# W2's broadcast rows kept in PSUM, layer 3's statistics from ScalarE, and a new order of the first microseconds, in a four-layer residual kernel

## The chip, the cores and the metric

The kernel runs on one core of a Trainium2 chip. The metric is the device time of one execution in microseconds; the time before is the median of 8 runs. TensorE is called PE, VectorE DVE, ScalarE ACT, GpSimd POOL and SyncE SP, as in the profile.

## What is computed

x has 128 batches of 128 x 512 numbers, adj is 128 x 128, all in float32. Four layers follow each other, each with a residual and a layer norm:

```
layer 0: y = adj @ x[b];  x = norm(x + y @ weight + bias)
layer 1: q, k, v = x Wq^T, x Wk^T, x Wv^T;  rel = adj^T * (q k^T)
         rel = rel / |rel| (by row);        x = norm(x + rel @ v)
layer 2: h = x W;  e = leaky(h a1 + (h a2)^T) * adj;  att = softmax(e)
         x = norm(x + elu(att @ h + beta h))
layer 3: A = adj @ x;  C = A + b;  pre[n, m] = A[m] + (C - A)[n]
         x = norm(x + max over m of relu(pre))
norm(x) = (x - mean) / sqrt(var + 1e-5) over the 512 features
```

Layer 3's maximum is one number per row: max(0, max_m A[m] + b). So layer 3 adds one number to each row of x, and then normalises the row.

## The kernel before

**Groups.** Four batches make a group (G = 4), and there are 32 groups (NG). Layer 1's q k^T is computed as x M x^T with M = Wq^T Wk, made once. The 512 x 512 products (y with weight, x with M, x with Wv^T, z with W, called y, m, v and z) are done for a whole group in seven steps in place of eight, with sums of blocks of both factors: `weight_blocks` (L143) makes the sums of the weights on DVE, once per weight; `left_factors` (L294) makes those of the activations on POOL, per group, four instructions; `product` (L339) issues the steps in the order 1, 2, 6, 5, 7, 3, 4 (ORDER, L290). Their results build up in three PSUM regions (REGION, L291): r0 takes steps 1, 6, 7, 4, r1 takes step 2, r2 takes steps 5 and 3. After each step, `out` (L353) reads the region: ACT copies it to its block of the result after steps 1, 6, 5 and 4, and DVE adds it to a block after 2, 7 and 3 (in the y product DVE adds all seven). A region's next step may not start before it has been read.

**PSUM.** There are eight banks of 128 x 512. Four take turns as `bank` (tag "ps", L82), for single matmuls and transposes: `p_y`, `p_xT`, `p_rel`, `p_o`, `p_s`, `p_eT`, `p_z`, `p_a` and those of the preparation. Four take turns as regions (tag "r", L350). `direct` (L700), the last group's z product, uses four "r" buffers too.

**Order.** All five engines run their instructions in the order of emission (InOrder, L18). The order is written out by hand: each piece is emitted with a time in slots (TABLE, L231), a group is 28 slots behind the one before, and the pieces are sorted by that number (L783). So the layers of neighbouring groups are interleaved: between the steps of one group's m product stand the `p_y` matmuls of the next group, and so on. FIRST (L248) and LAST (L250) replace rows for the first two and the last three groups.

**Around the change.** `dots` (L559) takes, for each batch, two dot products of every row of x2 (layer 1's x before its norm) with the rows W2 a1 and W2 a2: a DVE instruction `scr<-x,wa` that multiplies and accumulates. The rows, broadcast over the partitions, stand in SBUF as `wa` (L138), made by `prepare_rows` (L202) from transposes in PSUM and two ACT copies. `scale_dots` (L574) turns the dots into those of the normalised x, `d`, which `spread` transposes into `p_s`. `residual` (L545) precedes the dots, and `norm` (L375) follows: `ve` on DVE, the power -0.5 on POOL (`rstd`), `nmean` on DVE, and the scaling on ACT. `elu` (L716) does two DVE instructions (`x<-c,x` and `x<-m,x`) and the statistics for each batch.

Layer 3 (L747): `widen` is adj @ x on PE (`p_a`), `top` is the maximum over a row on DVE (`mx`), the bias and relu on DVE (`top<-mx,b_sb`), and the addition to x on ACT (`x<-x,top`). Then `stats` (L368), bn_stats and bn_aggr on DVE, and `norm`.

**The fill.** SP issues adj, four loads of the first x, Wq, Wk, Wv, a, beta, b; ACT issues the loads of weight (`w0_sb`), bias and W (`w2_sb`), L91 to L122. adj is transposed on PE and copied to `adjT` by ACT (L131). `biased` (L428) adds the bias to x on POOL, four instructions per group, ahead of the sums `s_y` of the y product. M is made by `prepare_qk` (L163), 16 matmuls of 128 x 512 in four banks with four ACT copies; `prepare_v` transposes Wv.

Of the kernel before, what the change touches and what calls it, by code (L numbers as in the profile page):

```python
# [13 lines left out]
EPS = 1e-5  # L14
# [15 lines left out]
def kernel(  # L30
# [41 lines left out]
    G = 4  # L72
    NG = B // G
    assert B % G == 0 and K == 4

# [3 lines left out]
    small = ctx.enter_context(tc.tile_pool(name="small", bufs=4))  # L79
    psum = ctx.enter_context(tc.tile_pool(name="psum", bufs=4, space=bass.MemoryType.PSUM))  # L80

    def bank(name):  # L82
        return psum.tile([P, D], FP, tag="ps", name=name)

# [20 lines left out]
    bias_sb = const.tile([P, D], FP)  # L105
    nc.scalar.dma_start(bias_sb, on_all(bias0, D))

# [7 lines left out]
    w2_sb = const.tile([P, K, D], FP)  # L115
    nc.scalar.dma_start(w2_sb, w2.rearrange("(k p) f -> p k f", p=P))
    a_sb = data.tile([P, 2, D], FP, tag="x3", name="a_sb")
# [9 lines left out]
    dve.memset(mhalf, -0.5)  # L127

    adjT = const.tile([P, P], FP)
    pt = bank("p_adjT")  # L130
    pe.transpose(pt[:, :P], adj_sb, ident)  # L131
    act.copy(adjT, pt[:, :P])
    adj_b = adj_sb[:, None, :].to_broadcast([P, G, P])
# [3 lines left out]
    wvT = const.tile([P, K, D], FP)  # L137
    wa = const.tile([P, 2, D], FP)  # L138
    wa_sum = const.tile([P, 2], FP)
    beta_i = const.tile([P, P], FP)  # L140
    beta_b = beta_i[:, None, :].to_broadcast([P, G, P])

    def weight_blocks(w, name, keep=0):  # L143


        def blk(kh, ch):
            return w[:, 2 * kh : 2 * kh + 2, H * ch : H * ch + H]

        t = const.tile([P, 3 + keep, 2, H], FP, name=f"t_{name}")
# [12 lines left out]

    def prepare_qk(c):  # L163

        pm = bank(f"p_m{c}")
        for e in range(K):
            pe.matmul(
                pm,
                wq_sb[:, e, c * P : (c + 1) * P],
                wk_sb[:, e, :],  # L170
                start=(e == 0),
                stop=(e == K - 1),
            )
        act.copy(m_qk[:, c, :], pm)
        if c == K - 1:
            bw["m"] = weight_blocks(m_qk, "m")

# [24 lines left out]
    def prepare_rows():  # L202

        for i in range(2):
            p = bank(f"p_wa{i}")
            for k in range(K):
                pe.transpose(
                    p[:, k * P : (k + 1) * P], col[:, i, k : k + 1].to_broadcast([P, P]), ident
                )
            act.copy(wa[:, i, :], p)  # L210
        dve.tensor_reduce(wa_sum, wa, AX.X, ALU.add, negate=True)
        dve.tensor_scalar(beta_i, ident, beta_sb, None, op0=ALU.mult)
# [14 lines left out]
    def row(at, step, n=G):  # L227
# [9 lines left out]
        move_rel=row(41.2, 0.1), inverse=[42.5], v=row(42, 1, 7), attend=row(50.6, 1),  # L237
        residual=row(51.0, 1), dots=row(54.2, 1.1), norm1=[55.2], scale=[58.8],
        apply1=row(65.4, 0.33),
# [7 lines left out]

    FIRST = {0: dict(turn=row(20.4, 0.3)), 1: dict(y=row(-9.5, 0.3), bias=row(-9.2, 0.3))}  # L248

# [89 lines left out]
    def product(at, name, mul, s, w, c, fresh, begin=None):  # L339
# [4 lines left out]
        def step(i):  # L344
            if i == 1 and begin is not None:
                begin()
            where = REGION[i]
            first = i in (1, 2, 5)
            if first:
                r[where] = psum.tile([P, 2, H], FP, tag="r", name=f"r{where}_{name}")  # L350
            mul(r[where], s["f"][i], bw[w][i], first)
# [262 lines left out]
    def layer2(g, t):  # L614
# [132 lines left out]
    def layer3(g, t):  # L747
        s = {}

        def widen(b):  # L750
            s["a", b] = bank(f"p_a_{g}_{b}")
            pe.matmul(s["a", b], adjT, x3[g][:, b, :], start=True, stop=True)

        def top(b):
# [3 lines left out]
            tp = small.tile([P, 1], FP, tag="top", name=f"top_{g}_{b}")  # L758
# [19 lines left out]
    emit(40.7, prepare_rows)  # L778
    emit(61.0, prepare_2)
    for g in range(NG):  # L780
# [33 lines left out]
```

## Time and profile before

| | us |
|---|---|
| median of 8 runs | 2235.38 (2233.30 to 2239.59) |
| the profiled execution | 2239.59 |
| its span, first to last instruction | 2237.4 |
| mean granted clock of PE | 0.996 |
| PE busy / DVE / ACT / POOL | 2185.5 / 1799.0 / 980.4 / 986.2 |
| DVE `scr<-x,wa` (dots), 256 | 288.0 busy, mean 1.176 |
| DVE bn_stats / bn_aggr, 512 each | 352.1 / 93.2 busy, mean 0.688 / 0.182 |
| DVE `top<-mx,b_sb`, 128 | 27.5 busy, mean 0.215 |
| DVE `ve<-mv`, 126 of 128x4 | 50.2 busy, mean 0.398 |
| ACT `x<-x,top`, 128 | 92.4 busy, mean 0.722 |
| ACT `x<-x,nmean,rstd`, 512 | 385.7 busy, mean 0.807 |
| ACT accumulator read, 128 of `sq` | 24.0 busy, mean 0.187 |
| PE `p_m` (Wq^T Wk), 32 records | 13.9 busy |

All durations are of one execution. A float32 matmul has two records on PE, a transpose one. Records overlap: the starts of two 128 x 256 records are 0.216 apart at full clock, so a step of eight takes 1.73; 128 x 128 records are 0.11 apart, and 0.21 at half clock. The group rows of the page give busy time and mean duration; the chain of waits gives start, length and name of what held up the end; the timeline gives start, length, engine and operation, and in brackets the idle time ahead of a row and what ended it.

### The profile page before, as it was taken

To read this page: it belongs to the slowest core of one execution; us is meant where nothing else is said; L and a number is where in the kernel's file an instruction comes from. 1 tells how busy PE (TensorE), PEld (TensorE's weight loads), DVE (VectorE), ACT (ScalarE), POOL (GpSimd) and SP (SyncE) were. 2 spreads that over 40 slices of the span, in tenths; PEclk is the share of its full clock that TensorE was granted. 3 is DMA by queue.
4 is the path that set the end of the run, shared out by engine and by line. 5 is a ranking of instruction groups with operands and counts; after the bars stand their busy time and mean duration, and the time that the engine had idled before them with its cause. 6 is when DMAs were issued, how large, how long until landed. Compare 5 with 4: busy or idle time off the path is not lost.

```text
span 2237.4 us, 31661 instructions
## 1 busy us (share of the span) xinstructions
PE 2185.5 (98%) x11073; PEld 1842.7 (82%) x11073; DVE 1799.0 (80%) x3534; ACT 980.4 (44%) x1936; POOL 986.2 (44%) x743
## 2 busy tenths in 40 slices
PE   7999999999999999999999999999999999999996
PEld 5888888888888888888888888888888888888873
DVE  4668888778888788888788888788887788887788
ACT  2224444454444444444444444444444444444535
POOL 3435454334444344554344553354543354443322
PEclk9999999999999999999999999999999999999998
DMA  4010222211222201222112222112222112221111
GB/s 166 25 33 18 58 58 62 62 21 47 59 60 62 62 14 54 57 62 62 43 30 57 57 62 62 41 29 59 57 62 62 38 30 59 59 62 43 20 29 57
DMA packets 333294, 115.15 MB, mean 51 GB/s; under 512 B 297424, under 2 KB 297552, under 8 KB 333136
## 3 DMA queue, kind: packets, MB, share of 16 engines
q1 hardware_dynamic: 331936, 110.77, 19.6%
q10 hardware_dynamic: 1200, 2.36, 0.3%
q8 instruction: 89, 1.46, 0.3%
q14 instruction: 69, 0.57, 0.1%
HBM read 39.65 MB, written 33.55 MB: 33 GB/s over the span
## 4 chain that ended last, share of the span: by engine, by line
PE 70%; DVE 24%; issue 3%; POOL 1%; ACT 1%; DMA 0%; DVEq 0%; ACTq 0%; POOLq 0%
PE r_v L26 17%; PE r_y L26 13%; PE r_z L26 13%; DVE x L26 7%; DVE scr L26 7%; PE r_m L26 6%; PE p_z L26 5%; PE p_o L26 5%; PE p_a L26 5%; PE p_rel L26 4%; DVE st L26 3%; DVE tT L26 2%; PE p_y L26 2%; DVE d L26 1%; DVE e L26 1%
## 5 line engine op out<-in xcount | busy, mean ns | idle before, releaser
L26 ACT ACTIVATE x<-x,nmean,rstd 128x512 f32<-128x512 f32 x512 | 385.7, 807 | 187.7 <-DVE nmean L26 187.6
L26 DVE BATCH_NORM_STATS2 st<-x 128x6 f32<-128x512 f32 x512 | 352.1, 688 | 56.6 <-ACT x L26 47.8
L26 DVE SCALAR_TENSOR_TENSOR scr<-x,wa 128x512 f32<-128x512 f32 x256 | 288.0, 1176 | 0.0
L26 POOL TENSOR_TENSOR rstd<-ve,mhalf 128x4 f32<-128x4 f32 (+1 forms) x134 | 145.4, 1085 | 285.8 <-DVE ve L26 279.8
L26 POOL TENSOR_TENSOR x<-x,bias_sb 128x512 f32<-128x512 f32 x128 | 193.9, 1525 | 74.0 <-PE p_y L26 73.3
L26 POOL TENSOR_TENSOR s_x<-xT 128x512 f32<-128x512 f32 x64 | 95.8, 1496 | 258.8 <-DMA xT<-xB 247.9
L26 ACT ACTIVATE x<-x,top 128x512 f32<-128x512 f32 x128 | 92.4, 722 | 229.6 <-DVE top L26 229.3
L26 DVE TENSOR_TENSOR x<-r_y,x 128x512 f32<-128x512 f32 x224 | 151.4, 676 | 27.0 <-PE r_y L26 26.9
L26 ACT COPY c<-r_z 128x512 f32<-128x512 f32 x124 | 71.9, 580 | 221.5 <-PE r_z L26 221.5
L26 ACT COPY yT<-p_y 128x512 f32<-128x512 f32 x128 | 75.1, 587 | 206.5 <-PE p_y L26 206.5
L26 PEld LDWEIGHTS p_y<-adjT,x 128*128 128x128 f32 x1024 | 135.8, 195 | 13.5 <-ACT adjT L26 5.5
L26 DVE SCALAR_TENSOR_TENSOR x<-p_o,rn,x 128x512 f32<-128x512 f32 x128 | 95.9, 749 | 59.9 <-PE p_o L26 56.0
L26 DVE SCALAR_TENSOR_TENSOR x<-m,x 128x512 f32<-128x512 f32 x128 | 132.8, 1037 | 13.6 <-DVE x L26 0.9
L26 PE MATMUL p_y<-adjT,x 128*128 128x128 f32 x1024 | 136.6, 278 | 6.8 <-ACT adjT L26 5.2
L26 PEld LDWEIGHTS p_z<-eT,x 128*128 128x128 f32 x1024 | 133.9, 192 | 8.4 <-DVE x L26 1.2
L26 PEld LDWEIGHTS p_rel<-xT,tT 128*128 128x128 f32 x1024 | 134.1, 191 | 7.4 <-DVE tT L26 0.8
L26 POOL TENSOR_TENSOR s_z<-zT 128x512 f32<-128x512 f32 x31 | 39.4, 1270 | 223.7 <-ACT zT L26 223.7
L26 PE MATMUL p_rel<-xT,tT 128*128 128x128 f32 x1024 | 134.9, 275 | 0.6 <-DVE tT L26 0.6
L26 PE MATMUL p_z<-eT,x 128*128 128x128 f32 x1024 | 134.8, 275 | 0.4 <-DVE x L26 0.4
L26 PE MATMUL p_a<-x,adjT 128*128 128x512 f32 x256 | 131.2, 597 | 3.6 <-ACT x L26 1.9
L26 ACT COPY tT<-r_m 128x512 f32<-128x512 f32 x128 | 75.6, 590 | 132.5 <-PE r_m L26 132.5
L26 PE MATMUL p_o<-v,relT 128*128 128x512 f32 x256 | 130.3, 593 | 0.0
(119 smaller groups left out, 5011.9 us busy)
## 6 DMA issues: line engine op xcount, KB each, us to landing
out_dram<-x SPq DMA_DIRECT2D x128, 256.0 KB, 2.5
x<-in_x_dram SPq DMA_DIRECT2D x31, 1024.0 KB, 5.8
xT<-xB SPq DMA_DIRECT2D x480, 64.0 KB, 2.3
relT<-relB SPq DMA_DIRECT2D x512, 16.0 KB, 1.8
w_sb<-in_L_gnn_weight_dram ACTq DMA_DIRECT2D x1, 1024.0 KB, 6.0
x<-in_x_dram SPq DMA_DIRECT2D x4, 256.0 KB, 7.5
wq_sb<-in_L_gnn_Wq_dram SPq DMA_DIRECT2D x1, 1024.0 KB, 11.4
wk_sb<-in_L_gnn_Wk_dram SPq DMA_DIRECT2D x1, 1024.0 KB, 14.4
```

What stands on the lines that cost most here:

```text
L26: return lambda *args, **kw: self.tc.keep_in_program_order(op(*args, **kw))
```

## The change

Three things are changed together.

1. PSUM is divided anew: three banks for "ps", two buffers for r0 (tag "r0"), one that r1 and r2 share (tag "r12"), and two banks that hold `wa` for good; `prepare_rows` transposes straight into it, without the copies. The dots read `wa` from PSUM. The dots, norm1 and the scale get earlier slots.
2. Layer 3's statistics: ACT squares the normalised x with an accumulated sum (`squares`), does the bias and relu (`top`, on 128 x 1) and sums x + top while it adds them. `spread` makes mean and variance of x + top from the two sums (the sum of squares belongs to an x whose mean is 0), with five DVE instructions and POOL's power. bn_stats and bn_aggr of layer 3 are gone.
3. The fill: eight identity products ahead of adj's transpose and eight behind the copy, which DVE does now; the loads of bias and W are issued by SP; M is made by `product` in seven steps, with Wq itself as the left factor; norm 0, turn and the bias adds of the first groups get other slots; `prepare_2` comes 12 slots earlier.

```diff
-    psum = ctx.enter_context(tc.tile_pool(name="psum", bufs=4, space=bass.MemoryType.PSUM))
+    psum = ctx.enter_context(tc.tile_pool(name="psum", bufs=1, space=bass.MemoryType.PSUM))
     def bank(name):
-        return psum.tile([P, D], FP, tag="ps", name=name)
+        return psum.tile([P, D], FP, tag="ps", name=name, bufs=3)
...
-    nc.scalar.dma_start(bias_sb, on_all(bias0, D))
+    nc.sync.dma_start(bias_sb, on_all(bias0, D))
...
-    nc.scalar.dma_start(w2_sb, w2.rearrange("(k p) f -> p k f", p=P))
+    nc.sync.dma_start(w2_sb, w2.rearrange("(k p) f -> p k f", p=P))
...
+    warm = bank("p_warm")
+    for i in range(WARM):
+        pe.matmul(warm[:, :P], ident, ident, start=True, stop=True)
     pe.transpose(pt[:, :P], adj_sb, ident)
-    act.copy(adjT, pt[:, :P])
+    dve.tensor_copy(adjT, pt[:, :P])
+    for i in range(WARM):
+        pe.matmul(warm[:, :P], ident, ident, start=True, stop=True)
...
-    wa = const.tile([P, 2, D], FP)
+    wa = psum.tile([P, 2, D], FP, tag="wa", name="wa")
...
-    def prepare_qk(c):
-        pm = bank(f"p_m{c}")
-        for e in range(K):
-            pe.matmul(pm, wq_sb[:, e, c * P : (c + 1) * P], wk_sb[:, e, :], ...)
-        act.copy(m_qk[:, c, :], pm)
-        if c == K - 1:
-            bw["m"] = weight_blocks(m_qk, "m")
+    def prepare_k():
+        bw["k"] = weight_blocks(wk_sb, "k", 1, "x2")
+    def prepare_m():
+        bw["m"] = weight_blocks(m_qk, "m")
...
         for i in range(2):
-            p = bank(f"p_wa{i}")
             for k in range(K):
                 pe.transpose(
-                    p[:, k * P : (k + 1) * P], col[:, i, k : k + 1].to_broadcast([P, P]), ident
-                )
-            act.copy(wa[:, i, :], p)
+                    wa[:, i, k * P : (k + 1) * P],
+                    col[:, i, k : k + 1].to_broadcast([P, P]),
+                    ident,
+                )
...
-        residual=row(51.0, 1), dots=row(54.2, 1.1), norm1=[55.2], scale=[58.8],
+        residual=row(51.0, 1), dots=[51.7, 53.8, 54.9, 55.6], norm1=[54.6], scale=[57.2],
...
-    FIRST = {0: dict(turn=row(20.4, 0.3)), 1: dict(y=row(-9.5, 0.3), bias=row(-9.2, 0.3))}
+    FIRST = {
+        0: dict(stats0=row(13.8, 0.02), norm0=[13.95], apply0=row(18.0, 0.1), turn=row(20.4, 0.3)),
+        1: dict(y=row(-9.5, 0.3), turn=row(20.3, 0.3), x_sums=row(22.5, 0.5)),
+    }
...
-                r[where] = psum.tile([P, 2, H], FP, tag="r", name=f"r{where}_{name}")
+                r[where] = psum.tile(
+                    [P, 2, H], FP, tag="r0" if where == 0 else "r12",
+                    name=f"r{where}_{name}", bufs=2 if where == 0 else 1,
+                )
...
-            s["c", b] = psum.tile([P, D], FP, tag="r", name=f"c_{g}_{b}")
+            s["c", b] = psum.tile([P, D], FP, tag="r0", name=f"c_{g}_{b}", bufs=2)
...
+        def squares(b):
...
+            act.activation(scr, x3[g][:, b, :], AF.Square, accum_out=s["sq"][:, b : b + 1])
         def top(b):
...
-            dve.tensor_scalar(tp, mx, b3_sb, 0.0, op0=ALU.add, op1=ALU.max)
-            act.activation(x, x, AF.Identity, bias=tp)
+            act.activation(tp, mx, AF.Relu, bias=b3_sb)
+            act.activation(x, x, AF.Identity, bias=tp, accum_out=s["sum"][:, b : b + 1])
+        def spread(i):
...
+            dve.tensor_scalar(s["mean", i], s["sum"][:, sl], -1.0 / D, None, op0=ALU.mult)
+            dve.tensor_tensor(d, s["mean", i], s["top"][:, sl], ALU.add)
+            dve.scalar_tensor_tensor(d, d, -1.0, d, op0=ALU.mult, op1=ALU.mult)
+            dve.tensor_scalar(s["sq"][:, sl], s["sq"][:, sl], 1.0 / D, EPS, op0=ALU.mult, op1=ALU.add)
+            dve.tensor_tensor(d, d, s["sq"][:, sl], ALU.add)
+            pool.tensor_tensor(s["r"][:, sl], d, mhalf[:, sl], ALU.pow)
+        def shift(i):
+            dve.tensor_tensor(s["mean", i], s["mean", i], s["r"][:, sl], ALU.mult)
...
+        for b in range(G):
+            emit(t["widen"][b] - 0.1, squares, b)
         each(t["top"], top)
-        each(t["stats3"], lambda b: stats(s, f"3_{g}", b, x3[g][:, b, :]))
-        norm(t["norm3"], t["apply3"], s, f"3_{g}", lambda: x3[g])
+        each(t["norm3"], spread)
+        for i in range(len(t["norm3"])):
+            emit(t["apply3"][i * n] - 0.1, shift, i)
+        each(t["apply3"], apply)
...
-    each(row(14.0, 1.0), prepare_qk)
-    each(row(18.0, 0.1), prepare_v)
+    emit(13.74, prepare_k)
+    qk = {"qT": wq_sb}
+    left_factors(row(12.0, 0.1), qk, "qT", "s_x", "q", 1)
+    product(row(14, 1, 7), "qk", by_rows, qk, "k", rows_of(lambda: m_qk), True)
+    emit(20.74, prepare_m)
+    each(row(21.0, 0.1), prepare_v)
     each(row(29.2, 1.8), prepare_dots)
     emit(40.7, prepare_rows)
-    emit(61.0, prepare_2)
+    emit(48.9, prepare_2)
```

More of the change, by code (lines that the diff above doesn't have):

```diff
@@ L73 @@
     NG = B // G
+    WARM = 8
     assert B % G == 0 and K == 4
@@ L141, with weight_blocks @@
     beta_b = beta_i[:, None, :].to_broadcast([P, G, P])
-    def weight_blocks(w, name, keep=0):
+    def weight_blocks(w, name, keep=0, where=None):
         def blk(kh, ch):
             return w[:, 2 * kh : 2 * kh + 2, H * ch : H * ch + H]
-        t = const.tile([P, 3 + keep, 2, H], FP, name=f"t_{name}")
+        if where is None:
+            t = const.tile([P, 3 + keep, 2, H], FP, name=f"t_{name}")
+        else:
+            t = data.tile([P, 3 + keep, 2, H], FP, tag=where, name=f"t_{name}")
         t2, t3, t4 = t[:, 0], t[:, 1], t[:, 2]
@@ L161, in prepare_0 @@
         bw["0"] = weight_blocks(w0_sb, "0")
-    def prepare_qk(c):
-        pm = bank(f"p_m{c}")
-        for e in range(K):
[L167 to L172, printed above, removed]
-            )
-        act.copy(m_qk[:, c, :], pm)
-        if c == K - 1:
-            bw["m"] = weight_blocks(m_qk, "m")
+    def prepare_k():
+        bw["k"] = weight_blocks(wk_sb, "k", 1, "x2")
+    def prepare_m():
+        bw["m"] = weight_blocks(m_qk, "m")
     def prepare_v(c):
@@ L349, in step @@
             if first:
-                r[where] = psum.tile([P, 2, H], FP, tag="r", name=f"r{where}_{name}")
+                r[where] = psum.tile(
+                    [P, 2, H],
+                    FP,
+                    tag="r0" if where == 0 else "r12",
+                    name=f"r{where}_{name}",
+                    bufs=2 if where == 0 else 1,
+                )
             mul(r[where], s["f"][i], bw[w][i], first)
@@ L752, in widen @@
             pe.matmul(s["a", b], adjT, x3[g][:, b, :], start=True, stop=True)
+        def squares(b):
+            if b == 0:
+                for key in ("sq", "sum", "top", "r"):
+                    s[key] = small.tile([P, G], FP, tag=f"l3_{key}", name=f"{key}_{g}", bufs=2)
+            scr = work.tile([P, D], FP, tag="scr3", name=f"scr3_{g}_{b}")
+            act.activation(scr, x3[g][:, b, :], AF.Square, accum_out=s["sq"][:, b : b + 1])
         def top(b):
@@ L757, in top, with apply @@
             dve.tensor_reduce(mx, s["a", b], AX.X, ALU.max)
-            tp = small.tile([P, 1], FP, tag="top", name=f"top_{g}_{b}")
-            dve.tensor_scalar(tp, mx, b3_sb, 0.0, op0=ALU.add, op1=ALU.max)
-            act.activation(x, x, AF.Identity, bias=tp)
+            tp = s["top"][:, b : b + 1]
+            act.activation(tp, mx, AF.Relu, bias=b3_sb)
+            act.activation(x, x, AF.Identity, bias=tp, accum_out=s["sum"][:, b : b + 1])
+        def spread(i):
+            sl = slice(i * n, i * n + n)
+            s["mean", i] = small.tile([P, n], FP, tag=f"l3_mean{n}", name=f"mean3_{g}_{i}")
+            dve.tensor_scalar(s["mean", i], s["sum"][:, sl], -1.0 / D, None, op0=ALU.mult)
+            d = small.tile([P, n], FP, tag=f"l3_d{n}", name=f"d3_{g}_{i}")
+            dve.tensor_tensor(d, s["mean", i], s["top"][:, sl], ALU.add)
[4 more added lines that the diff above has]
+        def shift(i):
+            sl = slice(i * n, i * n + n)
+            dve.tensor_tensor(s["mean", i], s["mean", i], s["r"][:, sl], ALU.mult)
+        def apply(b):
+            x = x3[g][:, b, :]
+            act.activation(
+                x,
+                x,
+                AF.Identity,
+                bias=s["mean", b // n][:, b % n : b % n + 1],
+                scale=s["r"][:, b : b + 1],
+            )
         def store(i):
```

## The prediction

> **What bounds the kernel now.** I read the page's busy line first, then the chain of waits, then the timelines of TensorE (PE) and VectorE (DVE) at the places that the chain names.
>
> ```profile
> PE 2185.5 (98%) x11073; PEld 1842.7 (82%) x11073; DVE 1799.0 (80%) x3534; ACT 980.4 (44%) x1936; POOL 986.2 (44%) x743
> ```
>
> PE is busy 98% of the span, so a faster DVE counts only where PE waits for it. The chain of waits (start, length, what) shows how often that is:
>
> ```profile
> 1373.91 3.45 PE r_z L26 x16
> ...
> 1440.72 3.45 PE r_z L26 x16
> 1454.52 3.04 DVE scr L26 x4
> 1458.71 3.58 DVE scr L26 x9
> 1476.91 1.97 PE r_y L26 x8
> ...
> 1508.47 3.45 PE r_z L26 x16
> ...
> 1575.28 3.45 PE r_z L26 x16
> ```
>
> Each `r_z` row opens the z product of one group of four batches. From 1373.91 to 1440.72, and from 1508.47 to 1575.28, a group takes 66.81 us, with PE alone on the chain. From 1440.72 to 1508.47 it takes 67.75, and the dot products (`scr`) stand in the chain. Over the 28 groups between the `r_z` rows at 221.65 and 2116.58 the mean is 67.68. So the steady part holds 1894.93 - 28 x 66.81 = **24.2 us** of waiting for a late DVE, and no more.
>
> DVE is late because of the dots (DVE timeline; start, us):
>
> ```profile
> 1455.80 1.75 DVE L26 SCALAR_TENSOR_TENSOR scr<-x,wa 128x512 f32<-128x512 f32 x1
> ...
> 1459.23 0.68 DVE L26 SCALAR_TENSOR_TENSOR scr<-x,wa 128x512 f32<-128x512 f32 x1
> ```
>
> The same instruction takes 1.75 while GpSimd (POOL) adds 512-wide tiles (`s_x` at that time) and 0.68 while it doesn't; the mean of 256 is 1.176.
>
> A second pair of timelines decides what fewer PSUM buffers cost. In the late group, then in the punctual one, DVE empties `r_m` twice (steps 7 and 3 of the m product):
>
> ```profile
> 1469.48 0.67 DVE L26 TENSOR_TENSOR tT<-r_m,tT 128x512 f32<-128x512 f32 x1
> ...
> 1474.18 0.66 DVE L26 TENSOR_TENSOR tT<-r_m,tT 128x512 f32<-128x512 f32 x1
> ```
> ```profile
> 1536.31 0.69 DVE L26 TENSOR_TENSOR tT<-r_m,tT 128x512 f32<-128x512 f32 x1 [0.19 <-PE r_m L26]
> ...
> 1540.62 0.66 DVE L26 TENSOR_TENSOR tT<-r_m,tT 128x512 f32<-128x512 f32 x1
> ```
>
> PE begins the second step of the next y product at 1473.90 and at 1541.65 (1.73 after the `r_y` rows start at 1472.18 and 1539.93). The second emptying ends at 1474.84 in the late group, 0.94 after that, and at 1541.28 in the punctual one, 0.37 before it. I compared these times in all groups: wherever DVE waited for PE at step 7, as at 1536.31, the margin is 0.36 to 0.38; elsewhere it is about -0.94 or -1.07.
>
> The fill, on PE and POOL:
>
> ```profile
> 8.79 6.29 PE L26 MATMUL p_y<-adjT,x 128*128 128x128 f32 x32 [5.24 <-ACT adjT L26]
> 14.92 3.62 PE L26 MATMUL r_y<-w_sb,yT 128*128 128x256 f32 x16
> 19.40 1.99 PE L26 MATMUL r_y<-t,s_y 128*128 128x256 f32 x8 [0.86 <-POOL s_y L26]
> ```
> ```profile
> 14.28 2.50 POOL L26 TENSOR_TENSOR x<-x,bias_sb 128x512 f32<-128x512 f32 x2 [0.35 <-PE p_y L26]
> 16.73 1.27 POOL L26 TENSOR_TENSOR s_y<-yT 128x512 f32<-128x512 f32 x1
> 18.08 1.26 POOL L26 TENSOR_TENSOR s_y<-s_y,yT 128x512 f32<-128x512 f32 x1
> ```
>
> PE starts late on `adjT`, runs at half clock until about 14, and then waits for POOL's sums, which stand behind the four bias adds.
>
> **What the Trainium skill says.** "SBUF — State Buffer", section "Who interferes with whom": a DVE instruction with two SBUF inputs contends with a POOL instruction that reads SBUF; one with at most one SBUF input, outside the two-port modes, doesn't. The trace agrees: 1.75 against 0.68 above, while `x<-r_y,x`, with one input in PSUM, has a mean of 0.676. "ScalarE: Activation LUTs", "Table sets: the hidden batching unit": relu is in every table set. The trace shows one table load (1.28) and no Relu; I charge no further load. "TensorE: Matmul & The Clock Gate", "What's actually happening": the clock rises after about 3.4 us of sustained work and falls after an idle window. The trace shows both, and a fall after only 2.1 us of waiting (116.18).
>
> **The change, part by part.**
>
> *Dots.* 8 per group. Bounds for x from SBUF, wa from PSUM: 0.61 (spacing of the undisturbed ones) and 0.75 (`x<-p_o,rn,x`, also one of each). I take 0.70: 8 x (1.176 - 0.70) = 3.8 us of DVE saved per group, where it is late. They also move forward: with dots(0) behind residual(0), dots(3) ends about 1459.5 in the first group shown, against 1464.5. The scale then waits for `rstd`, with step 2's emptying of m behind it on DVE (2.6 us of margin); the POOL op for `rstd` comes before the fourth `s_x` sum now and delays that by 1.1, 8 us ahead of need. So DVE reaches step 7's emptying before PE, as at 1536.31, in every group. Gain 24.2.
>
> *Layer 3's statistics.* Off DVE per group: 4 x (0.688 + 0.182) and 4 x 0.215 (`top`), 4.3; on: five small ops for one (`ve`), about +0.8. None is on PE's path here. On ScalarE (ACT): 4 squares, 4 accumulator reads with the adds and 4 relus. A square lies between 0.63 (`m<-c`) and 0.81 (`x<-x,nmean,rstd`) plus 0.09 of spacing per read; a 128x1 relu between 0.18 (128x128 and 512 forms extended to zero width) and 0.39 (128x128). With 0.80, 0.09 and 0.25, 4.6 us per group, 30.4 to 35 of 66.8. ACT is idle 1.3, 0.9 and 1.7 ahead of its first `top`, first zT copy and second `top` (before 1559.85, 1561.43, 1563.76); the first two squares fit there, and the others in the 3.0 before 1573.77. The relu waits for `mx` as the add to x does now, with the zT and v copies behind it, and DVE is no later with `mx`. Cost 0 in the steady part; if that cover were gone, each us of ACT lateness above the 0.89 margin at `r_v` would reach PE.
>
> *PSUM.* Banks from 4 to 3: in the steady part each bank is emptied at least 4.2 us before the third use after it. Regions r1 and r2 share one buffer: the margins are 2.6 (v), 2.5 (z), 0.77 (y), 0.5 (z to m, wider with early dots) and the 0.37 above. With a punctual DVE the cost is 0.
>
> *The fill.* adjT's copy leaves ACT, which was held by w2's DMA until 6.76; DVE does it in 0.3 before w0 lands at 6.7. PE can begin when x[0] lands, about 7.5 (now issued at 1.19, 6.4 later). bias and w2 on SP's queue put two issues of 0.4 to 0.5 and 1.25 MB ahead of group 1's load, issued at 13.8 and landed 12 later now; it is wanted at about 38, so that is hidden. The identity products (2 x 16 records at 0.21 cold) fill 1.4 to 7.5, and p_y runs warm, to 11.1. But bias now lands behind x[3], at about 10.4 (today the last x load, issued at 2.83, takes 7.5), and POOL still does 4 adds and 2 sums of 1.27: 18.1 for step 6, against 19.40. The warm clock itself is worth nothing. y ends at 26.75. Wq^T·Wk in 7 steps of 1.73 is 12.1 against 13.8; but its step 5 needs r12, whose reader stands on DVE behind four weight-block ops (2.9) and four statistics (3.3): out at 34.6, wanted at 31.9, a new wait of 2.7, with the rest of qk, group 1's y and the turn behind it on PE. The early norm and turn, and bias adds of group 1 out of POOL's way, win the rest: the first m step on sums starts about 53.1, against 56.26. Two long waits (3.5 and 2.7) can each lower the clock, 1.7 apiece, likelier than not: -2.2. Net gain 1 (from -2 to 4).
>
> *Groups 0 and 1, to 221.65.* Here PE loses 8.1 now: 2.1 for `p_s` at 116.18 and 1.7 more at half clock, 1.8 at 183.51, 1.0 at 91.21 and small ones. Shorter dots clear most; the shared region and the earlier prepare_2 ahead of the residuals put back some 3. Gain 5.
>
> *The tail* (from 2116.58). Earlier dots clear PE's waits before 2169 (some 4). From 2198 DVE works without rest to 2232; it sheds about 4.6 there, but ACT gets some 10 (8 squares, 8 relus, reads) on 17 of work in its last 24 and becomes the bound: it ends 3 later. Two direct products share `r0` now and wait 2, hidden by DVE. Earlier softmax +2.5. Net gain 4 (0 to 7).
>
> **Sum.** 24.2 + 1 + 5 + 4 = 34.2. The profiled execution took 2239.59 (span 2237.4 and 2.2 around it); it is the highest of eight and 4.2 above their median. From the median, 2235.4 - 34.2 = **2201**.
>
> **Rivals.** *Part of the gain comes back on PE*: ACT's lateness or the 0.37 margin costs 0.3 to 0.8 per group in 29 groups, 9 to 23 us: 2211 to 2226. For it: margins under 0.5. Against: PE waits nowhere in the punctual groups. Chance 0.22. *Slower*: the dots don't shorten, or something else keeps DVE a us late at step 7. Then the 24 stay, and since r1 and r2 share a buffer, PE also waits the 0.94 to 1.07, and about 0.07 of signalling, in each of 29 groups: 2235.4 - 10 + 29 = 2254. It decides from a lateness of 0.37. Against: every PSUM-fed DVE row here takes 0.68 to 0.75. Chance 0.09. *More gain*: no clock fall in the fill, and ACT's tail fits: 2190. Chance 0.07. The forecast, 2192 to 2211, has 0.62.
>
> A difference under about 0.2% (4.5 us) can't be told from none. Faster by more 0.88, within it 0.04, slower 0.08. The range 2191 to 2220 leaves out the slower case and the upper half of the first rival.
>
> **What will show it.** Right: `scr<-x,wa` near 0.70; `r_z` rows 66.8 apart throughout; no PE wait at y's second step; a PE wait of 2 to 3 us in the qk product for DVE `m_qk`; POOL sums setting `r_y<-t,s_y` at about 18; ACT without gaps in the last 15 us. Wrong: group times above 67, or new ACT table loads.

## The result, and the profile after

| | before | after |
|---|---|---|
| median, us | 2235.95 (32 runs) | 2223.78 (11 runs) |
| profiled execution, us | 2239.59 | 2223.52 |
| its span | 2237.4 | 2221.5 |
| DVE / ACT / POOL busy | 1799.0 / 980.4 / 986.2 | 1545.8 / 1102.3 / 914.0 |

The ratio is 0.9941 (95% interval 0.9932 to 0.9951): 12 us faster, where 34 were forecast, and above the range, which ended at 2220. The direction was right, the size was not. In the profiled executions the gain is 15.9 us of span. The profiled execution of before took 3.6 more than its median, so about 3.6 of these 15.9 belong to that one execution; a single trace can't say in which stage they lie.

The page after, its busy line, the chain that ended last by engine, and the row of the dots (busy us, mean ns):

```profile
PE 2177.2 (98%) x11129; PEld 1851.2 (83%) x11129; DVE 1545.8 (70%) x3298; ACT 1102.3 (50%) x2445; POOL 914.0 (41%) x747
...
PE 93%; DVE 3%; ACT 2%; POOL 1%; issue 1%; DMA 0%; SPq 0%; ACTq 0%; DVEq 0%; POOLq 0%
...
L26 DVE SCALAR_TENSOR_TENSOR scr<-x,wa 128x512 f32<-128x512 f32 x256 | 161.4, 675 | 0.0
```

The dots take 0.675 each (0.70 was taken), DVE is far from full, and the chain is PE's alone. PE's timeline shows the z products one period apart:

```profile
1497.91 3.62 PE L26 MATMUL r_z<-w_sb,zT 128*128 128x256 f32 x16
...
1564.72 3.62 PE L26 MATMUL r_z<-w_sb,zT 128*128 128x256 f32 x16
```

That is 66.81 through the whole steady part, with one exception (67.47): there PE waited 0.39 for DVE at y's second step, the place that the prediction watched. The timeline starts of the `r_z` rows divide the span into the prediction's own stages:

| stage | before | after | gain | forecast |
|---|---|---|---|---|
| to the first m step on sums | 56.26 | 54.67 | +1.6 | +1 |
| from there to group 1's `r_z` | to 221.49 | to 227.83 | **-7.9** | **+5** |
| the 28 groups after it | 1894.93 | 1871.39 | +23.5 | +24.2 |
| tail | 120.98 | 122.28 | **-1.3** | **+4** |
| sum | | | 15.9 | 34.2 |

The steady part and the fill came as forecast. Two terms did not: groups 0 and 1 are 12.9 off, the tail 5.3. PE's timeline after, where it waits in the early part (in brackets the idle time ahead and what ended it):

```profile
18.46 3.49 PE L26 MATMUL r_y<-t,s_y 128*128 128x256 f32 x8 [4.00 <-POOL s_y L26]
...
36.30 3.72 PE L26 MATMUL r_qk<-t_k,s_q 128*128 128x256 f32 x16 [2.27 <-DVE m_qk L26]
```
```profile
62.52 3.65 PE L26 MATMUL r_m<-s_x,m_qk 128*128 128x256 f32 x8 [5.85 <-DVE tT L26]
```
```profile
118.08 3.78 PE L26 MATMUL r_m<-s_x,m_qk 128*128 128x256 f32 x8 [4.34 <-DVE tT L26]
121.65 1.91 PE L26 MATMUL p_y<-adjT,x 128*128 128x128 f32 x8
```

The first two were forecast (18.1 and 2.7). The other two were not. Both are step 5 of the m product, in group 0 and in group 1, waiting for DVE to empty the buffer that r1 and r2 now share. Behind each the clock is down: eight records take 3.65 and 3.78 in place of 1.89. The two waits are 10.2, the slow records behind them 4.5 (1.8 at the first; 1.9 and 0.9 more in the `p_y` row at the second): together 14.7, more than the 12.9 that are missing in this stage.

Why DVE is late at the first, in DVE's timeline before and then after (start, length):

```profile
46.74 1.62 DVE L26 TENSOR_TENSOR t_v<-wvT 128x512 f32<-128x512 f32 x1 [1.31 <-ACT wvT L26]
...
51.66 1.75 DVE L26 TENSOR_TENSOR wvT<-wvT 128x512 f32<-128x512 f32 x1
53.33 1.75 DVE L26 SCALAR_TENSOR_TENSOR scr_wa<-w_sb,a_sb 128x512 f32<-128x512 f32 x1
...
56.68 0.68 DVE L26 TENSOR_TENSOR tT<-r_m,tT 128x512 f32<-128x512 f32 x1
```
```profile
52.06 1.43 DVE L26 TENSOR_TENSOR t_v<-wvT 128x512 f32<-128x512 f32 x1 [1.65 <-ACT wvT L26]
...
56.77 1.75 DVE L26 TENSOR_TENSOR wvT<-wvT 128x512 f32<-128x512 f32 x1
58.44 1.75 DVE L26 SCALAR_TENSOR_TENSOR scr_wa<-w_sb,a_sb 128x512 f32<-128x512 f32 x1
...
61.78 0.68 DVE L26 TENSOR_TENSOR tT<-r_m,tT 128x512 f32<-128x512 f32 x1
```

It is the same queue, 5.1 to 5.3 us later: Wv's four weight blocks, a pair of products for `wa`, then step 2's emptying. Before, the emptying ended 0.73 ahead of PE's step 5 (58.09). After, Wv's copies reach DVE 5.3 later, since the change moved `prepare_v` from slot 18 to slot 21, behind group 1's y and group 0's turn on PE. PE itself was 1.6 earlier. Nothing in the queue could catch up: each of these instructions, the emptying apart, has two SBUF inputs and runs beside POOL's adds, at 1.43 to 1.75 in place of 0.69 (the length of the same blocks in the run v_early below, where POOL is idle). "SBUF — State Buffer" in the Trainium skill, section "Who interferes with whom", says that such a pair contends; the trace agrees.

At the second wait, DVE's timeline after:

```profile
114.06 0.68 DVE L26 SCALAR_TENSOR_TENSOR scr<-x,wa 128x512 f32<-128x512 f32 x1
114.67 0.08 DVE L26 DVE_READ_ACCUMULATOR scr<-x,wa 128x1 f32 x1
114.67 2.46 DVE L26 SCALAR_TENSOR_TENSOR d<-mv,wa_sum,d 128x4 f32<-128x4 f32 x2
117.22 0.17 DVE L26 TENSOR_TENSOR d<-d,rstd 128x8 f32<-128x8 f32 x1
117.33 0.69 DVE L26 TENSOR_TENSOR tT<-r_m,tT 128x512 f32<-128x512 f32 x1
```

The change put only the scale (`d`, 2.6 us here) ahead of this emptying. The dots stood ahead of it before, too, and it was late then as well. The kernel before, PE's step 5 and DVE's emptying of step 2 in group 1:

```profile
107.83 1.89 PE L26 MATMUL r_m<-s_x,m_qk 128*128 128x256 f32 x8
```
```profile
112.25 0.68 DVE L26 TENSOR_TENSOR tT<-r_m,tT 128x512 f32<-128x512 f32 x1
```

The emptying ended 5.1 after the start of step 5, and PE didn't wait, since r1 and r2 had a buffer each. With one buffer for both, what is left of this lateness with shorter dots becomes a wait, and the scale adds to it. In the steady part DVE arrives in time, because PE has a z product of an older group between the first `p_o` and step 5. PE after, a steady group and then group 1:

```profile
1501.36 1.02 PE L26 MATMUL p_o<-v,relT 128*128 128x512 f32 x2
...
1521.29 1.89 PE L26 MATMUL r_m<-s_x,m_qk 128*128 128x256 f32 x8
```
```profile
102.11 3.77 PE L26 MATMUL p_o<-v,relT 128*128 128x512 f32 x8
```

From the first `p_o` to step 5 a steady group has 19.9 us, and the emptying is done 2.6 ahead of step 5. In group 1 no older group has a z product yet: PE was ready for step 5 at 113.74 (118.08 less the wait), 11.6 after `p_o`.

### The profile page after: what moved, and what is told of

Read it like the earlier page. It is cut to its first block, busy times and chain, and to the rows that moved or that the text cites. A ratio compares the mean times of both kernels' runs of the same rounds, so it can differ in the third digit from the quotient of the medians.

```text
span 2221.5 us, 31991 instructions
## 1 busy us (share of the span) xinstructions
PE 2177.2 (98%) x11129; PEld 1851.2 (83%) x11129; DVE 1545.8 (70%) x3298; ACT 1102.3 (50%) x2445; POOL 914.0 (41%) x747
## 3 DMA queue, kind: packets, MB, share of 16 engines
q8 instruction: 89, 1.46, 0.3%
## 4 chain that ended last, share of the span: by engine, by line
PE 93%; DVE 3%; ACT 2%; POOL 1%; issue 1%; DMA 0%; SPq 0%; ACTq 0%; DVEq 0%; POOLq 0%
PE r_y L26 17%; PE r_m L26 17%; PE r_v L26 17%; PE r_z L26 16%; PE p_z L26 5%; PE p_rel L26 5%; PE p_y L26 5%; PE p_o L26 5%; PE p_a L26 5%; DVE x L26 1%; ACT x L26 1%; DVE st L26 1%; PE p_eT L26 1%; PE p_s L26 1%; DMA bias_sb<-in_L_gnn_bias_dram 0%
## 5 line engine op out<-in xcount | busy, mean ns | idle before, releaser
L26 ACT ACTIVATE x<-x,nmean,rstd 128x512 f32<-128x512 f32 x384 | 288.5, 808 | 120.9 <-DVE nmean L26 120.9
L26 DVE BATCH_NORM_STATS2 st<-x 128x6 f32<-128x512 f32 x384 | 263.9, 687 | 8.8
L26 POOL TENSOR_TENSOR x<-x,bias_sb 128x512 f32<-128x512 f32 x128 | 171.5, 1342 | 124.9 <-PE p_y L26 114.8
L26 POOL TENSOR_TENSOR s_x<-xT 128x512 f32<-128x512 f32 x64 | 81.9, 1280 | 273.0 <-DMA xT<-xB 223.3
L26 DVE SCALAR_TENSOR_TENSOR x<-m,x 128x512 f32<-128x512 f32 x128 | 114.4, 894 | 112.5 <-ACT m L26 102.5
L26 POOL TENSOR_TENSOR rstd<-ve,mhalf 128x4 f32<-128x4 f32 (+1 forms) x99 | 98.6, 996 | 195.1 <-DVE ve L26 189.9
L26 DVE SCALAR_TENSOR_TENSOR scr<-x,wa 128x512 f32<-128x512 f32 x256 | 161.4, 675 | 0.0
L26 DVE STREAM_TRANSPOSE xB<-x 128x512 f32<-128x512 f32 x120 | 81.2, 696 | 109.0 <-ACT x L26 98.1
L26 DVE TENSOR_REDUCE mx<-p_a 128x1 f32<-128x512 f32 x128 | 88.3, 691 | 69.9 <-PE p_a L26 69.9
L26 PE MATMUL r_m<-s_x,m_qk 128*128 128x256 f32 x512 | 124.7, 387 | 10.2 <-DVE tT L26 10.2
```

The source lines that it names most:

```text
L26: return lambda *args, **kw: self.tc.keep_in_program_order(op(*args, **kw))
```

## The experiments

All are edits of the changed kernel, each timed four to six times together with the kernel before on the same chip. The intervals of the ratios are 0.1 to 0.2% to either side (2 to 4 us), so a single edit of 2 us is judged by its trace. Differences in us are from 2223.78, the changed kernel's median, which was not timed again beside them; they are uncertain by about 2 us. For groups 0 and 1 the traces give a surer measure, the time from the first m step on sums to group 1's `r_z`: 165.23 before and 173.16 after.

| run | median | ratio to before |
|---|---|---|
| wa_sbuf | 2275.92 | 1.0192 (1.0169 to 1.0215) |
| stats3_dve | 2223.23 | 0.9944 (0.9930 to 0.9958) |
| r1_own | 2218.91 | 0.9926 (0.9913 to 0.9938) |
| order_g0 | 2221.90 | 0.9936 (0.9924 to 0.9949) |
| v_early | 2218.53 | 0.9916 (0.9898 to 0.9934) |
| order_g1 | 2217.95 | 0.9925 (0.9911 to 0.9939) |
| g1_dots | 2215.87 | 0.9908 (0.9890 to 0.9925) |
| no_warm | 2222.01 | 0.9933 (0.9917 to 0.9948) |
| bias_dve | 2218.82 | 0.9920 (0.9902 to 0.9937) |
| all_mended | 2203.08 | 0.9856 (0.9838 to 0.9873) |
| stats3_last | 2222.05 | 0.9941 (0.9925 to 0.9956) |
| all_mended_tail | 2199.65 | 0.9839 (0.9822 to 0.9855) |
| direct_banks | 2226.78 | 0.9960 (0.9947 to 0.9972) |
| direct_third | 2225.23 | 0.9945 (0.9928 to 0.9962) |
| best2 | 2200.41 | 0.9842 (0.9829 to 0.9856) |
| best2_bias | 2201.11 | 0.9844 (0.9831 to 0.9858) |
| best_third | 2200.29 | 0.9834 (0.9816 to 0.9853) |

### What freed the steady part

**wa_sbuf**: `wa` in SBUF again.

```diff
-    wa = psum.tile([P, 2, D], FP, tag="wa", name="wa")
+    wa = const.tile([P, 2, D], FP)
```

> W2's rows are copied to SBUF, as before; all else is the changed kernel, the shared buffer of r1 and r2 and the early dots too. Theory A (PSUM is what shortens the dots, and the shorter dots are what freed the steady part): scr<-x,wa back at 1.0 to 1.2 us, DVE late at step 7 again and the shared buffer adds to it: 2245 to 2270 us. Rival C (the 4.3 us that layer 3's statistics take off DVE and the earlier dots suffice without PSUM): 2230 or less, with groups still 66.8 us apart.

The page's row of the dots, then PE's timeline in a steady group:

```profile
L26 DVE SCALAR_TENSOR_TENSOR scr<-x,wa 128x512 f32<-128x512 f32 x256 | 288.5, 1171 | 0.0
```
```profile
1350.95 1.99 PE L26 MATMUL r_m<-s_x,m_qk 128*128 128x256 f32 x8 [2.02 <-DVE tT L26]
```

The dots are back at 1.171, and the loss is 52, more than the 46 at which the expected range ended; 46.6 of it lies in the steady part of the trace (1918.02 in place of 1871.39). The wait sits at step 5 of the m product, in all 28 steady groups, 0.33 to 2.32 long. So the prediction's slower rival (a late DVE makes PE wait, and all the more since r1 and r2 share) is a true mechanism. The size is near the 24 + 29 = 53 that it was given, but the place is another, step 5 and not y's second step, where PE waits once (0.38). The change escapes it because the dots do shorten. Theory A. What the dots' earlier slots add to the gain is not shown: no run puts them back with `wa` in PSUM.

**stats3_dve**: layer 3's statistics by bn_stats and bn_aggr in all groups, as before.

```diff
-        each(t["top"], top)
-        each(t["norm3"], spread)
...
+        each(t["top"], old_top)
+        each(t["stats3"], lambda b: stats(s, f"3_{g}", b, x3[g][:, b, :]))
+        norm(t["norm3"], t["apply3"], s, f"3_{g}", lambda: x3[g])
```

> Layer 3's statistics are taken on DVE again in all groups (bn_stats, bn_aggr, add and max for top); all else is the changed kernel. Theory A (the dots alone freed the steady part; layer 3's work falls into DVE's idle stretches there): groups stay 66.8 us apart, and only the tail moves, where DVE gets 7 us more and ScalarE 11 less: 2221 to 2227. Rival C (the 3.5 us per group that layer 3 took off DVE are needed for step 5 or step 7 of the m product): groups at 67.2 or more, 2235 and above.

2223.23, with `r_z` rows 66.81 apart from first to last. In the steady part this half of the change buys nothing and costs nothing, as the prediction said of it. Theory A.

### Groups 0 and 1

**r1_own**: r1 of these two products in the banks that `wa` takes later.

```diff
+            if i == 2 and name in ("qk", "m_0"):
+                t = psum.tile([P, 2, D], FP, tag="wa", name=f"r1_{name}")
+                r[where] = t[:, 0, :].rearrange("p (j h) -> p j h", j=2)
```

> Region r1 of Wq^T Wk and of group 0's m product lies in the two banks that wa takes only later, so that these two products don't share one buffer between r1 and r2; nothing is reordered. Theory A (the shared buffer, met by a late DVE, costs the 15 us that the early part fell short): the wait of 5.85 us at 62.5 and the one of 2.27 at 36.3 go, with the half clock after the first (1.75): about 2214 us, and the wait of 4.34 at 118 stays. Rival B (DVE is too late in the fill whatever the buffers): PE only waits some us later in the same product, for the emptying of r1 or the weight blocks of v, and the time stays at 2221 or above.

4.9 less, between the two. The waits at 36 and at 62.5 are gone, and PE meets a late DVE three steps on, at step 4, which needs step 7's emptying:

```profile
63.69 3.39 PE L26 MATMUL r_m<-xT,t_m 128*128 128x256 f32 x8 [4.03 <-DVE tT L26]
```

So in group 0 the shared buffer is where PE waits, but not why DVE is late, and one more buffer can't take the lateness up.

**order_g0**: Wv's blocks and the products for `wa` behind that emptying.

```diff
-            bw["v"] = weight_blocks(wvT, "v")
-    each(row(29.2, 1.8), prepare_dots)
+    emit(34.0, prepare_wv)
+    each([29.8, 33.8, 34.9, 36.1], prepare_dots)
```

> Only DVE's order in the fill changes: Wv's weight blocks and the first products for wa stand behind step 2's emptying of group 0's m product, not ahead of it; the buffers stay shared. Theory A: the wait of 5.85 us at 62.5 and the half clock after it (1.75) go, the other two waits stay: about 2216 us. Rival B (DVE is too late in any order, or the later weight blocks hold up the v product): 2221 or above, with a new wait of 3 us or more in group 0's m or v product.

```profile
70.54 3.12 PE L26 MATMUL r_y<-t,s_y 128*128 128x256 f32 x8 [4.70 <-DVE x L26]
```

1.9 less, as rival B had it, though the new wait came in group 1's y product and not in group 0's m or v: the work that was put behind the emptying now stands ahead of that product. From 54 to 72 DVE has this work to do beside POOL's adds, in whatever order. That leaves doing it earlier.

**v_early**: only that.

```diff
-    each(row(21.0, 0.1), prepare_v)
+    each(row(18.0, 0.1), prepare_v)
```

> One number is undone: Wv's transposes (prepare_v) stand at 18.0 again, ahead of group 1's y and group 0's turn on PE, not at 21.0 behind them; the buffers stay shared. Theory D (the wait at 62.5 comes from the move of prepare_v: its copies reach DVE at 52 in place of 46.7, so that the weight blocks and the first products for wa meet GpSimd's adds and stand ahead of step 2's emptying of group 0's m product): the weight blocks run at about 0.69 each near 42 to 46, step 2's emptying waits for PE alone, the wait of 5.85 and the half clock behind it are gone and nothing takes their place: about 2216 us. Rival B (DVE has too much work between 50 and 72 whatever the order, as where the blocks were only put later): a new wait of 4 us or more in group 0's m or group 1's y product, 2220 or above.

DVE's timeline, then PE's:

```profile
44.89 0.69 DVE L26 TENSOR_TENSOR t_v<-wvT 128x512 f32<-128x512 f32 x1 [7.73 <-ACT wvT L26]
...
56.92 0.68 DVE L26 TENSOR_TENSOR tT<-r_m,tT 128x512 f32<-128x512 f32 x1
```
```profile
56.50 1.99 PE L26 MATMUL r_m<-s_x,t_m 128*128 128x256 f32 x8 [0.90 <-POOL s_x L26]
58.33 1.89 PE L26 MATMUL r_m<-s_x,m_qk 128*128 128x256 f32 x8
```

The blocks take 0.69 in a stretch in which POOL is idle, and step 5 follows step 6 without a gap, with the buffers still shared. 5.3 less in place of 7.8, since Wv's transposes stand ahead of y and turn on PE again and the sums `s_x` come 1.8 later. Theory D: the move of one preparation step is what cost here. The stage of groups 0 and 1 takes 165.11 in this trace.

**order_g1**: the scale alone behind group 1's emptying (57.8), and `prepare_2` back at 61.

> For group 0 alone scale_dots goes just behind step 2's emptying of group 1's m product, and w2's weight blocks (prepare_2) go back to where the kernel before had them, behind the dots. Theory A: the wait of 4.34 us at 118 and the half clock behind it (3) go: about 2216.5 us, the waits at 36 and 62 stay. Rival B (the time is only shifted, as the score row p_s then waits for the scaled dots, 2 us as in the kernel before): 2220 to 2222.

```profile
114.06 1.99 PE L26 MATMUL r_m<-s_x,m_qk 128*128 128x256 f32 x8 [1.67 <-DVE tT L26]
...
125.75 1.99 PE L26 MATMUL r_y<-w_sb,yT 128*128 128x256 f32 x8 [1.46 <-DVE tT L26]
```

5.8 less, which lies between the two forecasts and decides for neither. The wait at step 5 falls from 4.34 to 1.67, so the scale made up 2.7 of it; the other 1.7 is what stood ahead of the emptying before the change, too. A wait of 1.46 comes up at the next emptying, behind w2's blocks, which take 1.64 to 1.75 there against 0.69 where the change has them. Moving `prepare_2` forward was no fault. In the changed kernel it is done before group 1's residuals, and DVE then waits 1.14 for PE:

```profile
103.25 0.75 DVE L26 SCALAR_TENSOR_TENSOR x<-p_o,rn,x 128x512 f32<-128x512 f32 x1 [1.14 <-PE p_o L26]
```

**g1_dots**: the last two dots and the scale of group 0 behind that emptying.

```diff
+               dots=[51.7, 53.8, 57.75, 57.8], scale=[57.9]),
```

> For group 0 alone the dots of batches 2 and 3 and scale_dots stand behind step 2's emptying of group 1's m product (57.75 to 57.9); w2's weight blocks stay where the change has them. Theory A (these ops, put ahead for the steady part, hold up that emptying in group 1): the wait of 4.34 us at 118 and the half clock behind it (3) go and no other comes: about 2216.5 us. Rival B (the lateness moves to the next emptying of r_m or to p_s, as with prepare_2 put back): a wait of 1.5 us or more remains, about 2219.

PE's timeline, steps 6, 5 and 7 of group 1's m product:

```profile
113.97 1.89 PE L26 MATMUL r_m<-s_x,t_m 128*128 128x256 f32 x8
115.70 1.05 PE L26 MATMUL p_y<-adjT,x 128*128 128x128 f32 x8
116.59 1.89 PE L26 MATMUL r_m<-s_x,m_qk 128*128 128x256 f32 x8
118.32 1.05 PE L26 MATMUL p_y<-adjT,x 128*128 128x128 f32 x8
119.21 1.89 PE L26 MATMUL r_m<-s_x,t_m 128*128 128x256 f32 x8
```

No wait, and none follows: 7.9 less. Theory A. The stage takes 165.53. The edit moves two dots and the scale, an order that neither kernel had.

### The fill

**no_warm**: WARM = 0, no identity products.

> The 16 identity products ahead of group 0's y are left out. The prediction said that the warm clock is worth nothing there, because GpSimd's sums set step 6: group 0's p_y runs at half clock and ends some 1.5 to 2 us later, step 6 still starts at 18 to 18.5, and the time stays within 1 us of 2223.8. Rival (the clock is worth what it saves): 2 us or more above, 2226.

```profile
7.06 5.53 PE L26 MATMUL p_y<-adjT,x 128*128 128x128 f32 x32 [3.63 <-DMA x<-in_x_dram]
...
18.45 1.99 PE L26 MATMUL r_y<-t,s_y 128*128 128x256 f32 x8 [2.41 <-POOL s_y L26]
```

`p_y` takes 5.53 in place of 3.81, and step 6 starts at 18.45 in place of 18.46: POOL's sums set it. The median is 1.8 less, outside the 1 us that was expected, but it can't be told from no difference. The warm clock is worth nothing there, as forecast.

**bias_dve**: group 0's bias adds on DVE.

> Group 0's four bias adds are DVE's, not GpSimd's; all else is the changed kernel. Theory (as the prediction has it, step 6 of group 0's y waits for GpSimd's sums behind the four adds): the sums start about 12, step 6 about 14.7 in place of 18.46, no half clock after it: up to 5 us less in y; but the qk product then waits longer for wk's blocks or its landing, so 2219 to 2222 in the whole. Rival (the first loads set the fill, not GpSimd): y's gain is all given back at the qk product, 2223 to 2224.

```profile
16.40 1.96 PE L26 MATMUL r_y<-t,s_y 128*128 128x256 f32 x8 [1.83 <-DVE x L26]
```

5.0 less by the medians, just under the theory's 2219 to 2222; in the trace PE is 1.9 ahead of the changed kernel at the first m step on sums and 2.5 at the last `r_z`. Step 6 starts at 16.40, behind DVE's adds, 2.1 earlier, where the theory had 14.7: the adds still wait for the bias and start at 11.02. The clock doesn't fall after step 6; in this trace it falls later, behind the wait in qk. The theory has the direction and not the time of step 6.

### The sum

**all_mended**: v_early, g1_dots, bias_dve, and group 0's layer 0 statistics at 15.8 in place of 13.8.

> Four edits of the order together: prepare_v at 18.0; group 0's last dots and scale behind step 2's emptying of group 1's m product; group 0's bias adds on DVE; group 0's layer 0 statistics behind step 2's emptying of the qk product. If the early loss is the sum of these waits: 5.3, 7.9 and 5.0 (as measured one by one) and 2.3 for qk's wait off 2223.8, 2203. Rival (one wait hides the next in the fill, as where Wv's blocks were put later): 2208 or above.

2203.08, 20.7 less. The spans of the two traces differ by 17.7: 1.7 in the fill, 14.5 in groups 0 and 1 (158.70 in place of 173.16), and 1.6 in the tail, where the clock didn't fall this time. So the waits of groups 0 and 1 don't hide each other. With both gone, this stage is 6.5 below the kernel before, where the prediction had 5. The gain in the fill is a new one; the forecast had had no error there. The edits are order alone: instructions moved, and four adds on another engine.

### The tail

**stats3_last** and **all_mended_tail**: layer 3's statistics of the last group on DVE (the edit of stats3_dve with `g == NG - 1`), alone and on all_mended.

> Only the last group's layer 3 statistics are DVE's again. Theory T (ScalarE sets the end: it works without a gap from 2197 to 2218): 4 squares with reads (3.2), 4 relus and 4 reads (1.9) leave it, DVE has 4.2 us idle there, the end comes 2 to 4 us earlier: about 2221. Rival (DVE or the chain of one batch through p_a, top, statistics and the last apply sets the end): 2223 to 2227.

> The same four edits, and the last group's layer 3 statistics on DVE. Theory T: 2 to 4 us below the run without the last edit. Rival: the same or above it.

The medians fall by 1.7 and 3.4; the first can't be told from nothing. The traces can be compared from the last group's first `p_eT` to the end of the span: 47.2 after (2174.31 to 2221.5), 45.6 in all_mended, 42.6 in all_mended_tail, 42.7 before. Between the first two the difference is the clock. `p_z` behind the same waits of 1.72 and 0.47, after and in all_mended:

```profile
2175.22 1.81 PE L26 MATMUL p_z<-eT,x 128*128 128x128 f32 x8
```
```profile
2159.08 1.06 PE L26 MATMUL p_z<-eT,x 128*128 128x128 f32 x8
```

Between all_mended and all_mended_tail it is ACT's work, 3.0. stats3_last shows the same with the clock down: 44.3 against the 47.2 after, 2.9 less. Theory T.

**direct_banks**: the third and fourth direct product in `wa`'s two banks, as one tile.

> Only the last group's direct products change: the third and fourth take the two banks that wa no longer needs, so that the four don't share r0's two. Theory U (the wait of 1.81 us ahead of the third product, 2189.5, which the prediction took for hidden by DVE, reaches the end): the wait goes, p_a starts 1.8 earlier after p_eT, the time falls 1.5 to 2 us: about 2222. Rival V (ScalarE or DVE sets the end, as the prediction said, so the wait is hidden): the wait goes and the waits of p_a grow by as much: 2223 to 2224.

2226.78, outside both ranges. ACT waited until both products in the tile were done before it read the first, a wait of the edit's own, so this run decides nothing. A second form of the edit doesn't have that wait:

**direct_third**: the third product takes r12's buffer.

```diff
-            s["c", b] = psum.tile([P, D], FP, tag="r0", name=f"c_{g}_{b}", bufs=2)
+            s["c", b] = psum.tile([P, D], FP, tag="r12" if b == 2 else "r0", ...)
```

> Only the third of the last group's direct products changes: it takes r12's buffer, free by then, in place of one of r0's two; each product keeps a buffer of its own, so that its readers wait for it alone. Theory U (the wait of 1.81 us ahead of the third product reaches the end): the wait goes and the time falls 1.5 to 2 us, to about 2222. Rival V (the wait is hidden, as the prediction said): the wait goes, the waits of p_a for ScalarE and DVE grow by as much: 2223 to 2224.

The tail after, then with the edit:

```profile
2189.49 7.13 PE L26 MATMUL c<-w_sb,zT 128*128 128x512 f32 x16 [1.81 <-DVE x L26]
2196.46 4.46 PE L26 MATMUL p_a<-x,adjT 128*128 128x512 f32 x10
2202.34 1.95 PE L26 MATMUL p_a<-x,adjT 128*128 128x512 f32 x4 [1.42 <-ACT x L26]
2208.68 1.28 PE L26 MATMUL p_a<-x,adjT 128*128 128x512 f32 x2 [4.39 <-DVE mx L26]
```
```profile
2190.04 7.03 PE L26 MATMUL c<-w_sb,zT 128*128 128x512 f32 x16
2196.91 4.80 PE L26 MATMUL p_a<-x,adjT 128*128 128x512 f32 x10
2204.14 2.84 PE L26 MATMUL p_a<-x,adjT 128*128 128x512 f32 x4 [2.42 <-ACT x L26]
2211.22 2.05 PE L26 MATMUL p_a<-x,adjT 128*128 128x512 f32 x2 [4.24 <-DVE mx L26]
```

The wait of 1.81 is gone and `p_a` starts 2.1 earlier after the first `p_eT`. But the wait for ACT grows, and from that `p_eT` (2176.84) to the end it is 47.3 against 47.2, with the clock down in both. In both, ACT works without a gap to the end from 22.8 after the first `p_eT`, so it sets the end. The median, 2225.23, lies 1.5 above the changed kernel's, outside both ranges, and can't be told from it. By the traces it is rival V: the wait was hidden, as the prediction said.

**best2**, **best2_bias**, **best_third**: all_mended_tail with the edit of direct_banks; that with bias loaded by ACT's queue; all_mended_tail with the edit of direct_third.

> All five edits that helped (prepare_v, group 0's dots, bias adds, statistics of layer 0, last group's layer 3 statistics on DVE) and the banks for the direct products: by theory U 1.5 to 2 us below the 2199.65 without the banks: 2198; by rival V 2199 to 2200.

> The same, and bias is loaded on ScalarE's queue as in the kernel before, not on SP's. If bias's landing behind the x loads still holds up group 0's y (step 6 at 15.8 to 17.6 with the adds on DVE), step 6 starts 0.9 to 2.5 us earlier: 2196. Rival (w0's transfer ahead of it on that queue makes it land no earlier): no change, 2198.

> The same edit on the version with the five edits that helped (2199.65). Theory U: about 2198. Rival V: 2199 to 2200.

2200.41, 2201.11 and 2200.29 beside 2199.65: nothing that can be told apart. With bias on ACT's queue it no longer holds up the y product (step 6 at 15.69, without a wait), but that is no earlier than all_mended_tail's 15.82. The best version is all_mended_tail, at 0.9839 (0.9822 to 0.9855), 24 us below the changed kernel.

## Why the prediction was wrong, step by step

- **Steady part, right.** 23.5 in place of 24.2, and by the step it named: dots of 0.675 (0.70), DVE punctual in all groups but one, groups of 66.81. wa_sbuf and stats3_dve show that it takes the dots in PSUM and not layer 3.
- **Layer 3 on ACT, right.** ACT gained 3.8 us per group (4.6 forecast): a square 0.624 (0.80 taken), its read 0.19, the relu 0.294 (0.25). The trace has one table load (1.28), as before: the relu needed none, as "ScalarE: Activation LUTs" in the Trainium skill, section "Table sets: the hidden batching unit", says of it.
- **Fill, right** in the sum (+1.6 for +1) and in the steps that were looked at: step 6 at 18.46 (18.1), the wait in qk 2.27 (2.7), the warm clock worth nothing. One of the two clock falls that it allowed for came. The other parts of the new fill (the loads, the early norm and turn, M in seven steps) were not run apart.
- **"Groups 0 and 1, to 221.65 ... Gain 5": the step that failed.** It measured -7.9. Gain 5 was 8.1 less some 3, and the 3 is the term that was wrong: "the shared region and the earlier prepare_2 ahead of the residuals put back some 3". What it stood for measured 14.7, two waits of 5.85 and 4.34 and half clock behind both, all at the shared buffer; the 8.1 came as 6.8. The prediction gives margins for steady groups only (2.6 for this emptying) and no working for the 3. In group 0 the sharing alone would have been free: the emptying was 0.73 early before. But `prepare_v`, three slots on, brings four weight blocks and the emptying behind them 5.1 to 5.3 later, and the prediction doesn't price that move at all; v_early takes it back, and with it 5.3. In group 1 the emptying was 5.1 late before the change, which cost nothing while r1 and r2 had a buffer each. With the shorter dots 1.7 of that is left (order_g1), and the earlier scale adds 2.7. g1_dots takes that wait away, and with it 7.9. prepare_2, which the prediction blamed, is free where it is.
- **"The tail ... Net gain 4": too high by 5.3.** ACT's term was right (3 forecast, 3.0 measured), and r0's two buffers were rightly called hidden. Too high were the earlier dots and the earlier softmax, 4 + 2.5: from the `r_z` row to the first `p_eT` the gain is 3.2 (78.28 to 75.09), and the softmax's own wait of 1.72 stands in both. And the clock fell once, 1.6. So 6.5 - 3 was forecast, and 3.2 - 3.0 - 1.6 came.
- **The rivals.** "Part of the gain comes back on PE" would have given the right time for a wrong reason: it spread 9 to 23 us over 29 groups, and of the steady groups only one lost any (0.66).
- **The base.** The prediction read its gains from an execution of 2239.59 and took them off a median of 2235.4. A gain that belongs to that execution alone is counted too much so, here up to 3.6 of the 22 that are missing; 12.9 are groups 0 and 1, and 5.3 the tail.
- **Open.** In which stage the profiled execution of before loses the 3.6 above its median; what decides whether the clock falls; and what the dots' earlier slots are worth alone.

## What to carry to other kernels

When buffers are taken away, check the margins not only in the steady state of the old trace but in the first and last rounds with the new order: walk each moved preparation step down the queues of all engines, and ask what now stands ahead of each emptying. A reader that was late without harm, since another buffer was free, becomes a wait when that buffer goes; so look for late readers in the old trace, and not for waits alone. An order that is right for the steady part is to be checked where the pipeline isn't full, since PE then comes sooner and DVE doesn't. And do a preparation step of this kind where POOL is idle: the same block took 0.69 there and 1.43 to 1.75 beside POOL's adds.

## What was not expected of the hardware

- The clock's fall is not settled by the length of the wait. Behind the same two waits in the tail (1.72 and 0.47) it fell in 10 of the 19 profiled executions, with that of after, v_early and g1_dots among them, and not in 9, with r1_own, order_g1 and all_mended among them; a fall there cost 1.1 to 1.6. In the fill it fell behind a wait of 4.00 (after), and not behind 3.77 (order_g1) or 3.40 (order_g0). "TensorE: Matmul & The Clock Gate" in the Trainium skill, section "What's actually happening", has it fall after an idle window of about 3.4 us, and says that the window runs free; here it fell after waits shorter than that, so the measurement differs from the page on the length. A window that runs free would fit the chance in it, but no run here shows what decides.
- Two DVE instructions on 128x4, `d<-mv,wa_sum,d`, took 2.46 together beside POOL's adds (the scale in group 1, after) and 0.34 at 2169.97 in direct_banks, where POOL was idle.
